# The first MLP layer of a perceiver block computed by Strassen's scheme

## The chip, the cores and the metric

The kernel runs on one core of one Trainium2 chip. The metric is the device time of one execution in microseconds (us). A core has five engines with queues of their own: TensorE (PE) multiplies matrices and writes to PSUM, with its weight loads shown apart as PEld; VectorE (DVE) and ScalarE (ACT) do elementwise work and read PSUM; GpSimd (POOL) does elementwise work in SBUF and issues gathering DMAs; SyncE (SP) issues the plain DMAs. The program writes out one list of instructions for each of them, and in the trace each engine takes its list in order: an instruction that waits holds up all that stand behind it on its engine.

## The reference

All data is float32. Thirty-two batches have 32 query rows of 512 each, and 257 context rows each.

```python
x = x + xattn(layernorm(x), ctx)          # 1: cross attention
x = x + attn(layernorm(x))                # 2: linear attention and an MLP
x = x + ffn(layernorm(x))                 # 3: sum of 8 adapters
# 1: K_hat = cos((ctx @ Wk + bk) @ Wr + br); softmax(Q @ K_hat.T) @ V
# 2: q = x @ Wq; features elu(q) + 1; msg = linear attention @ Wm
x = x + layernorm(msg) * g1 + b1
mlp = relu(msg @ W1) @ W2                 # W1: 512 x 1024, W2: 1024 x 512
x = x + layernorm(mlp) * g2 + b2
# 3: x @ (sum of weights[k] * W[ids[k]]).T + bias, W[i]: 512 x 512
```

`msg @ W1` is the product that the change touches. It has 1024 rows (32 batches of 32), an inner size of 512 and 1024 columns.

## The kernel before, in words

The 1024 query rows are eight groups of 128 rows (four batches each), called g = 0 to 7. The program is written out as 96 **slots**, numbered 8w + u for w in 0 to 11 and u in 0 to 7 (L1130 to L1156). Each slot emits a main piece, and around it pieces from two hand-written plans: `ahead` (L1063) puts a call in front of the slot's main piece and `at` (L1060) behind it. Since every queue is in order, these lists set the order on all engines; each slot's pieces also sit in the queues of DVE, ACT, POOL and SP.

The main pieces are: slots 0 to 63, the keys of the cross attention, two batches per four slots; 64 to 71, the first MLP layer for groups 0 to 3 (`hidden`, L969); 72 to 79, the second layer for these groups (`mlp`, L989); 80 to 87 and 88 to 95 the same for groups 4 to 7. Behind the main pieces, each group's own chain is strewn over some 30 slots: `q_*` (layer norm and query projection), `a_*` (attention, with `a_values` the value projection `xa` and `a_norm` the next layer norm), `b_*` (linear attention: `b_q`, `b_feat`, `b_turn_f`, `b_pairs`, `b_msg`, `b_merge`, `b_turn_m2`), then `mlp_norm` and `f_*`. The last group's chain lies in slots 64 to 80.

Between layers, a 128x512 result must be transposed. For groups 0 to 6 `move` (L261) sends it through four SP DMAs of 64 KB into a `moved` tile, and DVE transposes that in 32x32 blocks (`turn_moved`, L272); the last group goes over PE (`turn`, L245).

**Keys.** Two batches' keys are one product of a 512x512 matrix and a 512x512 matrix, and `pair_unit` (L560) computes it by Strassen's scheme in Winograd's form: seven products of 256x256 blocks instead of eight. `product` (L513) is one of them, four matmuls of 128x128 by 128x256 (in the trace eight instructions: every float32 matmul shows as two). Sums of weight blocks stand in `s_in` (made once, L481), sums of context blocks (`y_sum`, L498) in a tile `sums`, and partial results in a tile `parts`. Three PSUM banks take turns (`z_tile`, L113): bank a collects P1, P6, P7 and P4 one after the other, and is copied out to `parts` in between, so each product waits for a copy made one product earlier.

**First MLP layer.** `hidden(half, f)` computes 128 of the 1024 columns for 512 rows: four matmuls of 128x128 by 128x512 into one bank, then one ReLU on ACT into a tile of the pool `kh` (six buffers, which held the keys). The input `m2T[half]` holds the four groups' `m2` transposed. `m2T[1]` holds the key sums `s_in` until the last keys are done. W1 lies in two tiles `w1_0` and `w1_1` of the pool `stage` (three buffers; the other is the adapters' sum), loaded by SP in slots 34 to 42 and 63 to 66 (L1122 to L1127).

**Adapters.** `adapter_load(m)` (L666) gathers half an adapter, 512 KB, by POOL into buffers of the old context tiles; `adapter_add(m)` (L684) adds it, weighted, to `acc` on DVE; `adapter_move` and `adapter_turn` transpose the sum into `wff`, in the buffer of `wkr` (the product of Wk and Wr); `f_times` (L1041) uses it.

Of the kernel before, what the change touches and what calls it, by code (L numbers as in the profile page):

```python
# [9 lines left out]
F32 = mybir.dt.float32  # L10
I32 = mybir.dt.int32
AF = mybir.ActivationFunctionType
ALU = mybir.AluOpType
# [13 lines left out]
def tile_perceiver_block(  # L27
# [35 lines left out]
    nc = tc.nc  # L63
    P = 128
    B, S, D = x.shape
    SK = y.shape[1]
    DC = D // P
# [7 lines left out]
    NG = B // GB  # L75
# [3 lines left out]
    HALF = NG // 2  # L79
# [109 lines left out]
    weights = {}  # L189
# [133 lines left out]
    for e in range(DC):  # L323
# [11 lines left out]
        if e == 3:  # L335

            ps = tr_tile("phase_parts").rearrange("p a n -> p (a n)")
            for a in range(DC):
# [5 lines left out]
                    stop=True,  # L344
# [136 lines left out]
    def key_sums():  # L481

        (w11, w12), (w21, w22) = w_in
        s1, s2, s3, s4 = s_in
        nc.vector.tensor_tensor(s1, w21, w22, ALU.add)
        nc.vector.tensor_tensor(s2, s1, w11, ALU.subtract)
        nc.vector.tensor_tensor(s4, w12, s2, ALU.subtract)
        nc.vector.tensor_tensor(s3, w11, w21, ALU.subtract)
        sums = stage.tile([P, 3, 2, K0], F32, tag="stage", name="sums")
        parts = stage.tile([P, 4, 2, K0], F32, tag="stage", name="parts")  # L490
        pair_tiles["sums"] = [sums[:, i] for i in range(3)]
        pair_tiles["parts"] = [parts[:, i] for i in range(4)]

    def y_blocks(b):
        ya, yb = turned_y[b], turned_y[b + 1]
        return (ya[:, :2, :], yb[:, :2, :]), (ya[:, 2:, :], yb[:, 2:, :])

    def y_sum(b, i):  # L498

        if b >= B:  # L500
            return
        (y11, y12), (y21, y22) = y_blocks(b)
        t1, t2, t4 = pair_tiles["sums"]
# [462 lines left out]

    hid = {}

    def hidden(half, f):  # L969

        if f % 2 == 0:
            hid[half, f // 2] = khp.tile(
                [P, 2, HALF * P], F32, tag="kh", name=f"hid_{half}_{f // 2}"
            )
        ps = z_tile(f"hid_ps_{half}_{f}")
        for c in range(DC):
            nc.tensor.matmul(  # L977
                ps,
                lhsT=weights[f"w1_{f // 4}"][:, c, (f % 4) * P : (f % 4 + 1) * P],
                rhs=m2T[half][:, c, :],  # L980
                start=(c == 0),
                stop=(c == DC - 1),
            )
        nc.scalar.activation(hid[half, f // 2][:, f % 2, :], ps, AF.Relu)  # L984
        flush_sines()

    mlp_ps = {}

# [71 lines left out]
    def at(w, u, f, *args):  # L1060
        plan.setdefault((w, u), []).append((f, args))

    def ahead(w, u, f, *args):  # L1063

        early.setdefault((w, u), []).append((f, args))

    for g in range(NG):
        for j in range(GB):
            at(g + (5 + j) // 8, (5 + j) % 8, load_plain, g, [j])
        at(g + 1, 1, load_last, g)  # L1070
        if g:
            ahead(g + 0, 0, q_stats, g)
            ahead(g + 0, 5, q_norm, g)
        ahead(g + 1, 0, q_turn, g)
        at(g + 1, 0, q_times, g)
        w = g + 1
        if g == NG - 1:
            steps = (a_scores, a_turn_p, a_sum, a_turn, a_values, a_norm, b_turn)
            steps += (b_q, b_feat, b_turn_f, b_pairs, b_msg, b_turn_msg, b_merge)
            for u, f in enumerate(steps):  # L1080
                at(w + (u + 1) // 8, (u + 1) % 8, f, g)
            at(w + 1, 7, b_stats, g)
            at(w + 2, 0, b_norm, g)
# [3 lines left out]
        if g < NG - 2:  # L1087
            pass
        else:
            steps.update({b_q: 10, b_pairs: 14, b_msg: 15, b_merge: 18})  # L1090
            first.update({b_feat: 12, b_turn_f: 14, b_turn_msg: 17, b_turn_m2: 21, b_stats: 20, b_norm: 21})
# [5 lines left out]
    at(6, 4, adapter_fetch)  # L1097
    at(7, 0, adapter_start)
    at(7, 3, adapter_bias_load)
    at(8, 2, adapter_bias)  # L1100
    for m in range(2 * NK):
        at((60 + m) // 8, (60 + m) % 8, adapter_load, m)
        ahead((64 + m) // 8, (64 + m) % 8, adapter_add, m)
    for c in range(OP):
        at((79 + c) // 8, (79 + c) % 8, adapter_move, c)
        ahead((81 + c) // 8, (81 + c) % 8, adapter_turn, c)
    for g in range(2, NG):
        at(g - 2, 3 if g == 2 else 2, load_x, g)
    for g in range(NG - 3):
        u = 72 + 2 * g + 1 if g < HALF else 88 + 2 * (g - HALF) + 1  # L1110
        steps = {mlp_norm: u + 1, f_stats: u + 2, f_norm: u + 3, f_turn: u + 5, f_times: u + 6}
        if g < HALF:
            u = 80 + 2 * g
            steps.update({f_stats: u, f_norm: u + 1, f_turn: u + 3, f_times: u + 5})
        for f, u in steps.items():
            if (f, g) != (f_times, HALF):
                at(u // 8, u % 8, f, g)
# [4 lines left out]
    for i in range(2):  # L1122
        src = aw1[:, i * D : (i + 1) * D]
        parts += [(f"w1_{i}", src, stage, "stage", [q]) for q in range(4)]
    at_units = (2, 3, 4, 4, 9, 10, 11, 12, 18, 19, 20, 26, 34, 35, 36, 42, 63, 64, 65, 66)
    for part, u in zip(parts, at_units):
        at(u // 8, u % 8, load_weight, *part)  # L1127
    for q in range(4):
        at(8, 3 + q, load_w2, q)
    for w in range(12):  # L1130
        for u in range(8):
            if (w, u) == (8, 0):
                last_fraction()
            for f, args in early.get((w, u), ()):
                f(*args)
            if w < 8:
                b = w * GB + u // 2
                if b == 1:
                    turn_quads(2 + u % 2)
                    load_quads(4 + u % 2)  # L1140
                    if u % 2:
                        y_sum(2, 1)
                        y_sum(2, 2)
                    keys(1, u % 2)
                elif b > 1:
                    pair_unit(w * GB + u // 4 * 2, u % 4)
            elif w == 8:
                hidden(0, u)
            elif w == 9:
                mlp(u // 2, u % 2)  # L1150
            elif w == 10:
                hidden(1, u)
# [73 lines left out]
```

## Time and profile before

| what | value |
|---|---|
| median of 3 runs (lowest, highest) | 532.01 us (531.39, 532.18) |
| profiled execution: its own time | 531.07 us |
| its span, first to last instruction | 529.3 us |
| granted TensorE clock | 1.000 |
| slots 0 to 63 (start of the span to first `hid_ps` matmul) | 346.6 us |
| first MLP layer, groups 0 to 3, with the pieces between | 346.6 to 400.5 us |
| second layer, groups 0 to 3, with the pieces between | 401.0 to 442.2 us |
| first layer, groups 4 to 7, with two `ff` pieces | 442.2 to 476.6 us |
| all 128 `hid_ps` matmul instructions, busy | 57.1 us |
| all 16 ReLUs on ACT | 9.5 us |
| DVE busy in 364 to 378 us / in 442 to 476 us | 5.34 of 14 / 15.72 of 34 us |
| DMA share in 346 to 364 us / in 364 to 378 us | 0.91 / 0.68 |

The page of a profile gives the engines' busy time, the chain of work that ended last (followed back from the last instruction), and the costliest groups of instructions: line, engine, operation, tile written <- tiles read, shapes, count | busy us, mean ns of one | idle time before them and what ended it. The timeline gives start, length, engine, line and operation, merged where like follows like. The name `w` stands for tiles with numbers cut off: `w1_0`, `w1_1` and `w2`.

### The profile page before, as it was taken

The page shows a single profiled execution, that of the slowest core. Times are in us where ns is not written, and L with a number is a line of the kernel's source. Part 1 is how long each engine was busy: PE and PEld are TensorE (multiplying, and loading weights), DVE is VectorE, ACT ScalarE, POOL GpSimd, SP SyncE. Part 2 cuts the span into 40 slices and gives each one's busy share as a digit, 9 for nine tenths or more (in the row PEclk, how much of TensorE's full clock was granted, in tenths as well). Part 3 has the DMA queues.
Part 4 walks back from the last instruction along what each step waited for, and adds up shares of the span by engine and source line. Part 5 has one row for each costly group of instructions (what it writes and reads, how often), then busy time and mean ns, then how long its engine had stood idle before and what let it go on. Part 6 is the DMA issues. An engine that isn't in the chain of part 4 may idle for free.

```text
span 529.3 us, 8651 instructions
## 1 busy us (share of the span) xinstructions
PE 523.7 (99%) x3231; PEld 339.0 (64%) x3231; DVE 361.8 (68%) x621; ACT 205.2 (39%) x405; POOL 145.9 (28%) x164
## 2 busy tenths in 40 slices
PE   8999999999999999999999999999999999999997
PEld 6587877767867766767687676664444444444444
DVE  1498888779877887887887798573535667524473
ACT  0154674574573464456447346443212101110000
POOL 0012111311310420331143043226115776311331
PEclk9999999999999999999999999999999999999999
DMA  7659986557346465453623532578636321211002
GB/s 205 159 142 231 257 199 225 151 149 240 97 127 171 166 167 171 148 169 94 230 83 93 176 129 82 178 193 192 194 120 198 93 62 48 59 40 61 20 20 79
DMA packets 83857, 74.33 MB, mean 140 GB/s; under 512 B 7828, under 2 KB 69792, under 8 KB 83816
## 3 DMA queue, kind: packets, MB, share of 16 engines
q1 hardware_dynamic: 80928, 64.06, 42.7%
q0 software_dynamic: 2864, 9.73, 6.4%
q8 instruction: 25, 0.41, 0.3%
q14 instruction: 16, 0.13, 0.1%
q10 hardware_dynamic: 24, 0.01, 0.0%
HBM read 58.03 MB, written 2.10 MB: 114 GB/s over the span
## 4 chain that ended last, share of the span: by engine, by line
PE 95%; DVE 2%; DMA 1%; SPq 0%; issue 0%; POOL 0%; ACT 0%; DVEq 0%; POOLq 0%
PE a L517 20%; PE hid_ps L977 11%; PE mlp L996 10%; PE b L517 9%; PE q L753 5%; PE ff L283 5%; PE bq L283 5%; PE m L283 5%; PE xa L283 5%; PE c L517 5%; PE sc L771 3%; PE av L802 3%; PE wkr L312 3%; PE msg L910 2%; DMA quads<-in_ctx_dram 1%; PE pa L888 1%
## 5 line engine op out<-in xcount | busy, mean ns | idle before, releaser
L977 PE MATMUL hid_ps<-m2T,w 128*128 128x512 f32 x128 | 57.1, 596 | 0.2 <-issue 0.2
L537 ACT ACTIVATE parts<-kh,rounder 128x512 f32<-128x512 f32 x60 | 43.2, 720 | 36.3 <-DVE kh L534 35.8
L996 PE MATMUL mlp<-w,hid 128*128 128x512 f32 x128 | 56.9, 594 | 0.0
L541 DVE SCALAR_TENSOR_TENSOR kh<-parts,kh 128x512 f32<-128x512 f32 x60 | 42.1, 701 | 9.0 <-ACT parts L537 8.9
L550 ACT ACTIVATE kh<-kh 128x512 f32<-128x512 f32 x60 | 36.3, 627 | 29.8 <-DVE kh L542 29.6
L977 PEld LDWEIGHTS hid_ps<-m2T,w 128*128 128x128 f32 x128 | 23.8, 190 | 29.6 <-issue 29.6
L996 PEld LDWEIGHTS mlp<-w,hid 128*128 128x128 f32 x128 | 23.8, 190 | 27.9 <-issue 27.3
L379 DVE STREAM_TRANSPOSE yT<-quads 128x1024 f32<-128x1024 f32 x31 | 38.2, 1232 | 2.3 <-DMA quads<-in_ctx_dram 2.3
L239 POOL TENSOR_TENSOR rstd_n<-ve_n,mhalf 128x1 f32<-128x1 f32 x16 | 11.1, 692 | 83.4 <-DVE ve_n L237 83.3
L753 PEld LDWEIGHTS q<-hT,wq_sb 128*128 128x128 f32 x256 | 29.8, 192 | 3.5 <-issue 2.6
L517 PE MATMUL a<-sums,wkr 128*128 128x256 f32 x120 | 29.2, 386 | 1.0 <-DVE kh L534 1.0
L984 ACT ACTIVATE hid<-hid_ps 128x512 f32<-128x512 f32 x16 | 9.5, 596 | 53.1 <-PE hid_ps L977 53.1
L753 PE MATMUL q<-hT,wq_sb 128*128 128x128 f32 x256 | 29.9, 275 | 0.0
L517 PE MATMUL a<-yT,m2T 128*128 128x256 f32 x120 | 29.6, 389 | 0.0
L239 POOL TENSOR_TENSOR rstd_x<-ve_x,mhalf 128x1 f32<-128x1 f32 x8 | 7.7, 963 | 78.3 <-DVE ve_x L237 78.3
L529 ACT ACTIVATE parts<-a,turn 128x256 f32<-128x256 f32 x60 | 25.0, 468 | 10.1 <-PE a L517 9.3
L517 PE MATMUL a<-yT,wkr 128*128 128x256 f32 x120 | 28.9, 384 | 0.0
L283 PE MATMUL bq<-awq_sb,bhT 128*128 128x512 f32 x64 | 28.8, 592 | 0.0
L283 PE MATMUL m<-awm_sb,msgT 128*128 128x512 f32 x64 | 28.8, 592 | 0.0
L283 PE MATMUL xa<-wv_sb,aoT 128*128 128x512 f32 x64 | 28.8, 592 | 0.0
L283 PE MATMUL ff<-wff,h2T 128*128 128x512 f32 (+2 forms) x80 | 28.6, 509 | 0.0
L517 PE MATMUL a<-sums,m2T 128*128 128x256 f32 x120 | 28.4, 379 | 0.0
(196 smaller groups left out, 980.4 us busy)
## 6 DMA issues: line engine op xcount, KB each, us to landing
quads<-in_ctx_dram SPq DMA_DIRECT2D x128, 128.0 KB, 3.3
plain<-in_ctx_dram SPq DMA_DIRECT2D x32, 512.0 KB, 4.1
moved_h<-h SPq DMA_DIRECT2D x52, 64.0 KB, 2.2
x<-in_x_dram SPq DMA_DIRECT2D x8, 256.0 KB, 4.0
last<-in_ctx_dram SPq DMA_DIRECT2D x32, 64.0 KB, 2.1
w<-in_L_attn_W_dram SPq DMA_DIRECT2D x8, 256.0 KB, 4.8
w<-in_L_attn_W_dram SPq DMA_DIRECT2D x4, 512.0 KB, 3.4
moved_ao<-ao SPq DMA_DIRECT2D x28, 64.0 KB, 2.2
```

What stands on the lines that cost most here:

```text
L239: nc.gpsimd.tensor_tensor(rstd, ve, mhalf, ALU.pow)
L283: nc.tensor.matmul(ps, lhsT=srcT[:, c, :], rhs=w[:, c, :], start=(c == 0), stop=(c == n - 1))
L312: nc.tensor.matmul(acc[c], lhsT=wkT[:, e, c * P : (c + 1) * P], rhs=wr_sb[:, e, :], start=(e == 0), stop=(e == DC - 1),)
L379: nc.vector.transpose(t.rearrange("p c (n k) -> p n c k", k=32), quads.pop(b))
L517: nc.tensor.matmul(ps[:, o, :], lhsT=w[:, c, o * P : (o + 1) * P], rhs=yb[:, c, :], start=start and o == 0 and c == 0, stop=stop and o == ...
L529: nc.scalar.activation(dst[:, o, :], ps[:, o, :], AF.Identity, bias=turn0[:, r : r + 1], scale=INV_2PI)
L537: nc.scalar.activation(w, u, AF.Identity, bias=rounder)
L541: nc.vector.scalar_tensor_tensor(u, w, ROUNDER, u, ALU.subtract, ALU.subtract)
L550: nc.scalar.activation(u, u, AF.Sin, scale=-TURN)
L753: nc.tensor.matmul(ps[:, e, :], lhsT=wq_sb[:, d, e * P : (e + 1) * P], rhs=hT[:, d, :], start=(d == 0), stop=(d == DC - 1),)
L977: nc.tensor.matmul(ps, lhsT=weights[f"w1_{f // 4}"][:, c, (f % 4) * P : (f % 4 + 1) * P], rhs=m2T[half][:, c, :], start=(c == 0), stop=(c ...
L996: nc.tensor.matmul(ps, lhsT=hT, rhs=weights["w2"][:, f // 2, f % 2, :], start=(f == 0), stop=(f == FC - 1),)
```

## The change

`hidden` is replaced by `hidden_unit(half, k, u)`: for each half of the rows and each half k of W1's columns (a 512x512 by 512x512 product), four slots hold seven products, two in each of u = 0, 1, 2 and one in u = 3. Results go through DVE additions and ReLUs in place. For this, sums of W1's blocks (`w1_sum`, four per k) and of the input's blocks (`m2_sum`, four per half) are made on DVE. `sums` and `parts` of the keys are kept, so the pool `stage` has only one buffer left, for W1's first half. W1's second half goes to two `kh` buffers that held the last keys (`w1_load`); the sums for k = 0 to `wq_sb`, which needs the last `q_times` to be over (moved from slot 64 to 60); the adapters' sum to `wkr`'s buffer, and `wff` to `awq_sb`. Names in order of the slots:

- `w1_sum(0, 1..4)` in slots 61 and 62; `m2_sum(0, 1..4)` in 63 and 64; all four `w1_load` in 66 (before: `w1_1` in 63 to 66); `w1_sum(1, 1..4)` in 67 and 68; `m2_sum(1, 1..4)` in front of 80.
- Group 7: `q_stats` 56 to 52, `q_norm` 61 to 57, `q_turn` and `q_times` 64 to 60, `b_stats` 79 to 82, `b_norm` 80 to 83.
- Group 6: `b_feat` 68 to 67, `b_turn_f` and `b_pairs` 70 to 69, `b_msg` 71 to 70, `b_turn_msg` 73 to 71, `b_merge` 74 to 73, `b_stats` 76 to 75, `b_norm` 77 to 76.
- Adapters: loads 60 to 75 become 59 to 62 and 66 to 77; additions 4 to 15 stay in 68 to 79; moves 79 to 82 become 79, 80, 80, 81. The bias product goes from 66 to 68.
- `f_stats`, `f_norm` and `f_turn` of groups 0 to 3 come one slot later; `f_times` 85, 87, 89, 91 become 85, 88, 91, 94.

```diff
+    def w1_load(q):
+        if q == 0:
+            for i in range(2, 4):
+                hidden_tile(0, i)
+            for i in range(2):
+                w1_late.append(khp.tile([P, 2, D], F32, tag="kh", name=f"w1_1_{i}"))
+        v = aw1[:, D:].rearrange("(q c i) n -> q i c n", q=4, c=DC)
+        for i in range(2):
+            nc.sync.dma_start(
+                out=w1_late[i][q * 32 : (q + 1) * 32, :, :], in_=v[q][:, 2 * i : 2 * i + 2, :]
+            )
...
+        if i == 1:
+            nc.vector.tensor_tensor(s1, w21, w22, ALU.add)
+        elif i == 2:
+            nc.vector.tensor_tensor(s2, s1, w11, ALU.subtract)
+        elif i == 3:
+            nc.vector.tensor_tensor(s3, w11, w21, ALU.subtract)
+        else:
+            nc.vector.tensor_tensor(s4, w12, s2, ALU.subtract)
...
+        def add(dst, ps, p):
+            nc.vector.tensor_tensor(dst, ps, p, ALU.add)
+            relus.append(dst)
+        if u == 0:
+            product(a, w11, y11, stop=False)
+            product(c, w12, y21)
+            nc.scalar.copy(part[0], a)
+        elif u == 1:
+            product(a, s2, t2, start=False, stop=False)
+            product(d, s1, t1, stop=False)
+            add(h[0][0], c, part[0])
+            nc.scalar.copy(part[1], a)
+            nc.scalar.copy(part[2], d)
+        elif u == 2:
+            product(a, s3, y12, start=False, stop=False)
+            product(d, s4, y22, start=False)
+            add(h[1][1], a, part[2])
+            add(h[0][1], d, part[1])
+        else:
+            product(a, w22, t4, start=False)
+            flush_relus()
+            nc.scalar.activation(h[1][0], a, AF.Relu)
+    def flush_relus():
+        while relus:
+            t = relus.pop(0)
+            nc.scalar.activation(t, t, AF.Relu)
...
-            ad["acc"] = stage.tile([P, OP * D], F32, tag="stage", name="acc")
+            ad["acc"] = one.tile([P, OP * D], F32, tag="wkr", name="acc")
...
-            ad["wff"] = one.tile([P, DC, D], F32, tag="wkr", name="wff")
+            ad["wff"] = weights["awq_sb"]
...
+            u = 8 * g + 8 if g < NG - 1 else 8 * g + 4
+            ahead(u // 8, u % 8, q_turn, g)
+            at(u // 8, u % 8, q_times, g)
```

More of the change, by code (lines that the diff above doesn't have):

```diff
@@ L492, in key_sums @@
         pair_tiles["parts"] = [parts[:, i] for i in range(4)]
+        pair_tiles["all_parts"] = parts
     def y_blocks(b):
@@ L502, in y_sum, with block_sum @@
         (y11, y12), (y21, y22) = y_blocks(b)
+        block_sum(y11, y12, y21, y22, i)
+    def block_sum(y11, y12, y21, y22, i):
         t1, t2, t4 = pair_tiles["sums"]
@@ L967, in tile_perceiver_block @@
     hid = {}
[L969 to L973, printed above, removed]
-            )
[L975 to L985, printed above, removed]
+    w1_late = []
@@ new lines, in w1_load, with w1_blocks @@
+    def w1_load(q):
[8 more added lines that the diff above has]
+                out=w1_late[i][q * 32 : (q + 1) * 32, :, :], in_=v[q][:, 2 * i : 2 * i + 2, :]
+            )
+    def w1_blocks(k):
+        if k:
+            halves = w1_late
+        else:
+            halves = [weights["w1_0"][:, 2 * j : 2 * j + 2, :] for j in range(2)]
+        return [[halves[j][:, :, i * 256 : (i + 1) * 256] for j in range(2)] for i in range(2)]
@@ new lines, in tile_perceiver_block, with w1_sum @@
+    w1_sums = {}
+    def w1_sum(k, i):
+        (w11, w12), (w21, w22) = w1_blocks(k)
+        if k not in w1_sums:
+            if k:
+                spare = tmp.tile([P, 1, D], F32, tag="round", name="w1_spare", bufs=1)
+                homes = [wq_sb[:, 3, :], pair_tiles["all_parts"][:, 3], spare[:, 0, :]]
+                homes[1] = homes[1].rearrange("p c n -> p (c n)")
+            else:
+                homes = [wq_sb[:, n, :] for n in range(3)]
+            s1, s2, s4 = [t.rearrange("p (c n) -> p c n", c=2) for t in homes]
+            w1_sums[k] = [s1, s2, w21, s4]
+        s1, s2, s3, s4 = w1_sums[k]
+        if i == 1:
[4 more added lines that the diff above has]
+            nc.vector.tensor_tensor(s3, w11, w21, ALU.subtract)
+        else:
+            nc.vector.tensor_tensor(s4, w12, s2, ALU.subtract)
@@ new lines, in m2_blocks, with m2_sum, hidden_tile, hidden_unit @@
+    def m2_blocks(half):
+        t = m2T[half]
+        return [
+            [t[:, 2 * i : 2 * i + 2, j * 256 : (j + 1) * 256] for j in range(2)] for i in range(2)
+        ]
+    def m2_sum(half, i):
+        (y11, y12), (y21, y22) = m2_blocks(half)
+        block_sum(y11, y12, y21, y22, i)
+    def hidden_tile(half, i):
+        hid[half, i] = khp.tile([P, 2, HALF * P], F32, tag="kh", name=f"hid_{half}_{i}")
+    def hidden_unit(half, k, u):
+        pt = pair_tiles
+        (w11, w12), (w21, w22) = w1_blocks(k)
+        (y11, y12), (y21, y22) = m2_blocks(half)
+        s1, s2, s3, s4 = w1_sums[k]
+        t1, t2, t4 = pt["sums"]
+        part = pt["parts"]
+        if u == 0:
+            for i in range(2):
+                if (half, 2 * k + i) not in hid:
+                    hidden_tile(half, 2 * k + i)
+            for i, key in enumerate("acb"):
+                t = z_tile(f"hid_{key}_{half}_{k}", (B // 2 - 1 + 2 * half + k + i) % 3)
+                pt[key] = t.rearrange("p (o k) -> p o k", o=2)
+        a, c, d = pt["a"], pt["c"], pt["b"]
+        h = [
+            [hid[half, 2 * k + i][:, :, j * 256 : (j + 1) * 256] for j in range(2)]
+            for i in range(2)
+        ]
+        def add(dst, ps, p):
+            nc.vector.tensor_tensor(dst, ps, p, ALU.add)
+            relus.append(dst)
+        if u == 0:
+            product(a, w11, y11, stop=False)
[12 more added lines that the diff above has]
+            add(h[0][1], d, part[1])
+        else:
+            product(a, w22, t4, start=False)
+            flush_relus()
+            nc.scalar.activation(h[1][0], a, AF.Relu)
@@ L987, in tile_perceiver_block @@
+    relus = []
+    def flush_relus():
+        while relus:
+            t = relus.pop(0)
+            nc.scalar.activation(t, t, AF.Relu)
     mlp_ps = {}
@@ L1065, in ahead, with at_slot, ahead_slot @@
         early.setdefault((w, u), []).append((f, args))
+    def at_slot(n, *args):
+        at(n // 8, n % 8, *args)
+    def ahead_slot(n, *args):
+        ahead(n // 8, n % 8, *args)
+    slots = dict(load0=59, load4=66, add0=64, add4=68, wff=81, f=81, ft=85, fd=3, w1_late=66, w1_later=66, w2=67, s0=61, s1=67, t1=63, t3=64, v1=80, v3=80, bias=68)
+    last = (65, 66, 67, 68, 69, 70, 71, 72, 73, 74, 75, 76, 77, 78, 82, 83)
+    six = dict(b_q=10, b_pairs=13, b_msg=14, b_merge=17, b_feat=11, b_turn_f=13, b_turn_msg=15, b_turn_m2=21, b_stats=19, b_norm=20)
     for g in range(NG):
@@ L1071, in tile_perceiver_block @@
         if g:
[L1072 to L1075, printed above, removed]
+            u = 8 * g if g < NG - 1 else 8 * g - 4
+            ahead(u // 8, u % 8, q_stats, g)
+            ahead((u + 5) // 8, (u + 5) % 8, q_norm, g)
+        u = 8 * g + 8 if g < NG - 1 else 8 * g + 4
+        ahead(u // 8, u % 8, q_turn, g)
+        at(u // 8, u % 8, q_times, g)
         w = g + 1
@@ L1079, in tile_perceiver_block @@
             steps += (b_q, b_feat, b_turn_f, b_pairs, b_msg, b_turn_msg, b_merge)
[L1080 to L1083, printed above, removed]
+            steps += (b_stats, b_norm)
+            for u, f in zip(last, steps):
+                at_slot(u, f, g)
             continue
@@ L1086, in tile_perceiver_block @@
         first = {a_turn: 7, a_norm: 9, b_turn: 10, b_feat: 13, b_turn_f: 14, b_turn_msg: 20, b_stats: 23, b_norm: 26, b_turn_m2: 31}
[L1087 to L1091, printed above, removed]
+        if g == NG - 2:
+            for names in (steps, first):
+                names.update({f: six.get(f.__name__, u) for f, u in names.items()})
         for f, u in steps.items():
@@ L1099, in tile_perceiver_block @@
     at(7, 3, adapter_bias_load)
-    at(8, 2, adapter_bias)
+    at_slot(slots["bias"], adapter_bias)
     for m in range(2 * NK):
-        at((60 + m) // 8, (60 + m) % 8, adapter_load, m)
-        ahead((64 + m) // 8, (64 + m) % 8, adapter_add, m)
+        at_slot(slots["load0"] + m if m < 4 else slots["load4"] + m - 4, adapter_load, m)
+        ahead_slot(slots["add0"] + m if m < 4 else slots["add4"] + m - 4, adapter_add, m)
     for c in range(OP):
-        at((79 + c) // 8, (79 + c) % 8, adapter_move, c)
-        ahead((81 + c) // 8, (81 + c) % 8, adapter_turn, c)
+        at_slot(slots["add4"] + 11 + (c + 1) // 2, adapter_move, c)
+        ahead_slot(slots["wff"] + c, adapter_turn, c)
     for g in range(2, NG):
@@ L1112, in tile_perceiver_block @@
         if g < HALF:
-            u = 80 + 2 * g
-            steps.update({f_stats: u, f_norm: u + 1, f_turn: u + 3, f_times: u + 5})
+            u = slots["f"] + 2 * g
+            steps.update({f_stats: u, f_norm: u + 1, f_turn: u + 3})
+            steps.update({f_times: slots["ft"] + slots["fd"] * g})
         for f, u in steps.items():
@@ L1121, in tile_perceiver_block @@
     parts += [("awm_sb", awm, None, None, [q]) for q in range(4)]
[L1122 to L1125, printed above, removed]
+    parts += [("w1_0", aw1[:, :D], stage, "stage", [q]) for q in range(4)]
+    at_units = (2, 3, 4, 4, 9, 10, 11, 12, 18, 19, 20, 26, 34, 35, 36, 42)
     for part, u in zip(parts, at_units):
@@ L1128, in tile_perceiver_block @@
     for q in range(4):
-        at(8, 3 + q, load_w2, q)
+        at_slot(slots["w2"] + q, load_w2, q)
+        at_slot(slots["w1_late"] if q < 2 else slots["w1_later"], w1_load, q)
+    for i in range(1, 5):
+        n = (i - 1) // 2
+        at_slot(slots["s0"] + n, w1_sum, 0, i)
+        at_slot(slots["s1"] + n, w1_sum, 1, i)
+        at_slot(slots["t3" if n else "t1"], m2_sum, 0, i)
+        ahead_slot(slots["v3" if n else "v1"], m2_sum, 1, i)
     for w in range(12):
@@ L1147, in tile_perceiver_block @@
             elif w == 8:
-                hidden(0, u)
+                hidden_unit(0, u // 4, u % 4)
             elif w == 9:
@@ L1151, in tile_perceiver_block @@
             elif w == 10:
-                hidden(1, u)
+                hidden_unit(1, u // 4, u % 4)
             else:
```

## The prediction

> **What bounds the kernel now.** I read the page's busy times first, then the chain that ended last, then the costliest groups.
>
> ```profile
> PE 523.7 (99%) x3231; PEld 339.0 (64%) x3231; DVE 361.8 (68%) x621; ACT 205.2 (39%) x405; POOL 145.9 (28%) x164
> ...
> PE 95%; DVE 2%; DMA 1%; SPq 0%; issue 0%; POOL 0%; ACT 0%; DVEq 0%; POOLq 0%
> ...
> L977 PE MATMUL hid_ps<-m2T,w 128*128 128x512 f32 x128 | 57.1, 596 | 0.2 <-issue 0.2
> ```
>
> PE is busy in 523.7 of 529.3 us and is 95% of the chain. In the first MLP layer it hardly idles (0.2 us), so PE work taken out there shortens the run, unless a wait takes its place. The granted clock is 1.000 throughout. The PE timeline gives the price of the old and the new shape:
>
> ```profile
> 327.92 1.89 PE L517 MATMUL a<-yT,wkr 128*128 128x256 f32 x8
> 329.65 1.89 PE L517 MATMUL c<-yT,wkr 128*128 128x256 f32 x8
> 331.38 1.89 PE L517 MATMUL a<-sums,m2T 128*128 128x256 f32 x8
> 333.10 1.89 PE L517 MATMUL b<-sums,m2T 128*128 128x256 f32 x8
> ...
> 442.22 20.76 PE L977 MATMUL hid_ps<-m2T,w 128*128 128x512 f32 x48
> 462.82 3.60 PE L283 MATMUL ff<-wff,h2T 128*128 128x512 f32 x8
> ```
>
> Starts count, since lengths overlap. Six old units last 462.82 - 442.22 = 20.60 us, 3.433 each; a product lasts (333.10 - 327.92) / 3 = 1.727 us.
>
> **1. The products.** Removed: 16 units of 3.433 = 54.93 us. Added: 2 halves x 2 k x 7 products = 28 of 1.727 = 48.36 us. On PE: **-6.57 us**. Weight loads rise from 128 to 224, 190 ns each by the group of L517, below the 216 ns between two instructions of a product, so they stay hidden.
>
> **2. Elementwise work.** DVE gets 16 sums at 0.68 (row `sums<-yT,sums` of L507: 677 ns) and 12 additions from PSUM at 0.69 (L534), 19 us. ACT gets 12 copies at 0.59 (7 us); ReLUs stay 16. The keys' loop already shows this cadence: a copy or an addition stands under the next product (1.73 us), and PE idles 1.0 us in all its 105 products. DVE has room: busy 5.34 of 14 us in 364 to 378, 15.72 of 34 us in 442 to 476. Cost on PE 0 while the queues run ahead; the places where they may not follow.
>
> **3. Start of slots 64 and 65.** `q_times(7)` (3.57 us) moves to slot 60, so slots 61 to 64 begin 3.57 us later and slot 65 at 357.1 as before. P6 there needs bank a copied out. That copy stands on ACT behind the Sin of the last keys, that behind DVE's f21. Walking DVE's queue with its rows (`b_stats` at 348.2, 1.0; two transposes, f22, the zsum reductions: 352.1; two new sums 1.4; f12 and f21 2.1), f21 ends near 355.5, Sin and copy (0.6 each) near 356.8. P6 follows at 357.15: margin 0.35. I take 0; bound 0 to 0.7, one sum.
>
> **4. `bq` of group 6.** Its input now comes late: `xa` of group 6 ends at 357.1 instead of 353.56 while `bq` stays at 367.1. Between: update 0.75, statistics 1.0, two new sums 1.6 (L511: 930 ns, and 683), `bh` 0.55: 361.0. Then four SP issues of 0.62 (2.49), the last issued at 362.9 and landed 2.2 later (median of `moved_bh`): 365.1; DVE, with one normalisation and the reductions of `sc` in front, transposes (1.1) until 366.9 at most, against 367.1. With the landing of 7.0 that the group had at 358 us, when the DMA share was 0.91, it would end at 371.0, late by 3.9; W1's second half no longer loads in that time. I take 0.2, range 0 to 3.9, nearer the median.
>
> **5. W1's second half: the new wait.** The old loads came in slots 63 to 66 and had until slot 68. The new ones must wait for the last keys to be read (`sc` ends at 363.6) and stand on SP behind what these lines show:
>
> ```profile
> 356.96 2.49 SPq L266 DMA_DIRECT2D moved_bh<-bh  x4
> 362.54 3.33 SPq L266 DMA_DIRECT2D moved_msg<-msgs  x4
> 365.91 2.08 SPq L168 DMA_DIRECT2D last<-in_ctx_dram  x4
> 368.03 0.90 SPq L201 DMA_DIRECT2D w<-in_L_attn_W_dram  x2
> ```
>
> So they start at about 368.1: eight issues of 0.45, the last at 371.3, 1.05 MB. PE reaches slot 68, which reads them, after `bq` and `tr_p` (370.85), P4 (1.73) and `av` (1.86) at **374.5**. Lower bound of the landing: 3.3 (median of 128 KB `quads`), 374.6, wait 0. Upper: 11.4, the longest of the trace (512 KB `plain` in 347 to 350 us, 2.5 MB together): 382.7, wait 8.2. Between them decides what else loads. POOL gathers half adapters at the same time:
>
> ```profile
> 366.80 2.12 POOL L957 TENSOR_TENSOR x<-x,n 128x512 f32<-128x512 f32 x1
> 369.08 0.98 POOL L676 DMA_INDIRECT adapter<-in_L_ffn_W_dram,ido  x1 [0.15 <-issue]
> 370.36 0.94 POOL L676 DMA_INDIRECT adapter<-in_L_ffn_W_dram,ido_odd  x1 [0.30 <-issue]
> ```
>
> After the change three (loads 4, 5, 6) can start at 369.1, 370.4, 371.7, 0.5 MB each; load 7 stands behind a normalisation of slot 69. At the 219 GB/s of 346 to 364 us (share 0.91), W1 plus half of the gathers (1.05 + 0.75 MB) takes 8.2 us: 376.3; at the 264 GB/s read in 370 to 375 us, 374.9. I take a wait of **1.5 us** (376.0). The sums for k = 1 follow on DVE by 377.4, P6 of slot 69 needs them after 381: covered. Behind the waiting sum on DVE stand `msgT` of group 5 (needed in slot 70) and an adapter addition: no reader on PE before 381.
>
> **6. `pa` of group 6**, one slot earlier, needs a transpose on DVE behind the bias copy and two sums: 0.69 x 3 + 1.1 = 3.2 us after `bff`, while PE has P6 and P5, 3.45. Margin 0.25; I take 0.2, range 0 to 1.3 (one adapter addition, 1.28, in between).
>
> **7. Second half, slots 80 to 87.** No foreign PE work lies between the products except one `ff`. From the end of `mlp` 3: statistics 1.1, t1 and t2 1.4: 2.5 us, P6 follows at 3.45. The addition that frees bank a for P4 (slots 83, 87) has 1.73 us from P7's end and takes 0.7; the transposes of `wff` (1.05 each) before it end by 8.6 where P7 ends at 8.65. Cost 0, up to 2 if POOL or a landing holds one of them.
>
> A rule of the Trainium skill speaks against these sums. The trace shows an adapter addition of L692 taking 2.62 us at 415.53, median 1.28, beside POOL's additions at 415.79 and 417.14. The page "SBUF — State Buffer", section "Who interferes with whom", says that a DVE instruction with two SBUF inputs and a GpSimd instruction that reads SBUF exclude each other for a whole instruction. By it, one POOL addition of 1.27 in front of t2 would turn the margin of 0.95 into a wait of 0.3; the forecast would be 527.6.
>
> **8. Adapters.** `acc` waits for P4 of slot 63, which DVE's f21 awaits anyway. Loads 7 to 15 have two slots instead of four; the last is issued near 431, lands 5.7 later (median), its addition ends near 438.5; moves (2.5 of issue, 2.2 landing) and transposes are done before `ff` 0 near 458. Cost 0; 0 to 2 if a landing takes 8.0. **The tail** from 476 on keeps its PE work, 0; a spaced-out `ff` 3 puts its output DMA (2.0) before `n2` of group 7, with 1.3 us to spare.
>
> **Sum**: -6.57 + 1.5 + 0.2 + 0.2 = -4.7 us on the profiled execution's 531.07 (span 529.3, 1.8 around it): 526.4. The median of the runs shown, 532.01, is 0.94 above that execution: **527.3 us**.
>
> **Rivals.**
> - *W1 lands in time* and every margin holds: -6.57, 532.01 - 6.6 = **525.4**. For it: 128 KB DMAs land in 3.3 and the 264 GB/s row leaves 0.4 us. Against: three gathers start in the same 3 us.
> - *The queues become the bound.* DVE and ACT do not keep up where margins are 0.2 to 0.4: points 3, 4, 6 and 7 cost half their upper ends, 0.35 + 1.95 + 0.65 + 1.0 = 3.95, on top of 1.5: 532.0 - 6.6 + 5.45 = **530.9**. For it: DVE was busy 18.7 of 20 us in 300 to 320. Against: PE was busy throughout those 20 us.
> - *Slower: W1's second half lands as late as `plain` did.* 11.4 us from the last issue is a wait of 8.2 in slot 68: 532.0 - 6.6 + 8.2 + 0.4 = **534.0**. It passes no change when the wait exceeds 6.2 us, a landing after 380.7. For it: 2.6 MB are wanted within 4 us, as then. Against: the earlier 2.5 MB were all plain loads in one queue, and here W1 is ahead of most of the gathers.
> - *It doesn't do what it says*: the compiled products could need the same PE time, if 256 columns cost more than half of 512. The keys' rows above (1.727 against 3.433 / 2 = 1.717) exclude it; no chance is given.
>
> **How the numbers follow.** Forecast 0.50, in time 0.28, queues 0.12, late W1 0.10. About 0.2% (1.06 us) is what a measurement of this kernel can tell from no change. The late case is slower in most of its spread (0.08) and same in 0.02; the queues case lies at the edge of no change: faster 0.06, same 0.05, slower 0.01. So faster 0.50 + 0.28 + 0.06 = 0.84, same 0.07, slower 0.09. The range: the in-time case less 0.4 of run-to-run spread, 525.0, to the queues case, 530.9; outside lie the late case and some of both ends, under 2 in 10.
>
> **What would show it.** Right: some 224 matmul instructions at the products' line in the hidden slots, spaced 216 ns; slot 72 near 399 and slot 80 near 439; one idle of PE of 0.5 to 3 us before the first product of k = 1 in half 0, released by the DMA of W1's second half; no idle over 0.3 us in slots 80 to 87. Wrong: PE waiting there for DVE or ACT instead, `bq` of group 6 waiting for its transpose, or W1 landing after 378.

## The result, and the profile after

The changed kernel took a median of 532.9 us (22 runs, 531.3 to 534.5), the kernel before on the same chip 531.85 us (22 runs, 530.9 to 532.7). The ratio is 1.0020, with a 95% interval of 1.0011 to 1.0029: slower by a little, where 527.3 us was forecast. The profiled execution after has a span of 531.7 us against 529.3 us, 2.4 us more. The kernel before ran again beside the experiments; each ratio below is against its runs on the same chip.

The page of the changed kernel: busy times, granted clock in 40 slices, and the engines' shares of the chain that ended last.

```profile
PE 520.0 (98%) x3327; PEld 359.2 (68%) x3327; DVE 380.2 (71%) x649; ACT 211.6 (40%) x417; POOL 145.9 (27%) x164
...
PEclk9999999999999999999999999999799999999999
...
PE 91%; DMA 4%; DVE 3%; SPq 1%; POOL 1%; issue 0%; ACT 0%; DVEq 0%; POOLq 0%
```

PE has 3.7 us less to do than before (523.7), not 6.6, in a longer span. One slice, at 372 to 385 us, has a clock of 0.7, and DMA has risen from 1% to 4% of the chain. The PE timeline of the same kernel shows where (start, length, engine, line, operation, tiles, shapes, count, and in brackets the idle time before it and what ended it):

```profile
370.82 1.89 PE L521 MATMUL hid_a<-sums,w 128*128 128x256 f32 x8
372.71 1.92 PE L806 MATMUL av<-plain,pT 128*32 128x512 f32 x16
381.15 3.75 PE L521 MATMUL hid_a<-m2T,w 128*128 128x256 f32 x8 [6.52 <-DMA w<-in_L_attn_W_dram]
384.70 2.35 PE L521 MATMUL hid_c<-m2T,w 128*128 128x256 f32 x8
386.88 0.60 PE L249 MATMUL tr_ao<-ident,ao 128*128 128x128 f32 x4
...
406.61 3.60 PE L1094 MATMUL mlp<-w,hid 128*128 128x512 f32 x8
...
447.81 1.89 PE L521 MATMUL hid_a<-m2T,w 128*128 128x256 f32 x8
...
466.80 3.60 PE L283 MATMUL ff<-awq_sb,h2T 128*128 128x512 f32 x8
470.24 1.89 PE L521 MATMUL hid_a<-m2T,w 128*128 128x256 f32 x8
...
475.42 3.60 PE L1094 MATMUL mlp<-w,hid 128*128 128x512 f32 x8
```

PE stood still for 6.52 us in slot 68, in front of the first product of k = 1 in half 0, until W1's second half landed. Then two products that last 1.73 us elsewhere took 384.70 - 381.15 = 3.55 and 386.88 - 384.70 = 2.18 us. The windows of two microseconds around it (time, PE busy with its count, granted clock, DMA share, GB/s) show why:

```profile
374.00:376.00 2.00, 0.63 (x8) 1.00 1.10 205
376.00:378.00 2.00, 0.00 (x0) 1.00 1.00 260
378.00:380.00 2.00, 0.00 (x0) 0.70 1.04 295
380.00:382.00 2.00, 0.85 (x2) 0.50 1.12 248
382.00:384.00 2.00, 2.00 (x6) 0.50 1.07 270
384.00:386.00 2.00, 2.00 (x7) 0.60 1.05 409
386.00:388.00 2.00, 2.00 (x11) 1.00 0.31 111
```

While PE stood, the clock fell to a half and came back at 385.6 us or so. The two products took 1.82 + 0.45 = 2.27 us more for it, all on the path. The DMA engines were full from 374 us on (share 1.00 and more). What filled them, by the DMA issues of this stretch (KB of each, median us from issue to landing, where the view has one):

```profile
w<-in_L_attn_W_dram SPq DMA_DIRECT2D x8, 128.0 KB, 7.7
w<-in_L_attn_W_dram SPq DMA_DIRECT2D x3, 512.0 KB, 6.9
last<-in_ctx_dram SPq DMA_DIRECT2D x4, 64.0 KB, 1.9
moved_f<-f SPq DMA_DIRECT2D x4, 64.0 KB
adapter<-in_L_ffn_W_dram,ido POOLq DMA_INDIRECT x2, 9.2
adapter<-in_L_ffn_W_dram,ido_odd POOLq DMA_INDIRECT x1, 9.5
```

The eight of 128 KB are W1's second half, the three of 512 KB are quarters of W2 (issued from 378.08 on). The start times are in SP's and POOL's timelines:

```profile
363.87 2.48 SPq L266 DMA_DIRECT2D moved_msg<-msgs  x4
366.70 1.73 SPq L168 DMA_DIRECT2D last<-in_ctx_dram  x4
368.55 3.64 SPq L985 DMA_DIRECT2D w<-in_L_attn_W_dram  x8
```

```profile
369.19 1.01 POOL L680 DMA_INDIRECT adapter<-in_L_ffn_W_dram,ido  x1 [0.16 <-issue]
370.50 0.94 POOL L680 DMA_INDIRECT adapter<-in_L_ffn_W_dram,ido_odd  x1 [0.30 <-issue]
371.75 0.94 POOL L680 DMA_INDIRECT adapter<-in_L_ffn_W_dram,ido  x1 [0.31 <-issue]
```

W1's first part was issued 0.6 us ahead of the first gather and its last beside the third; all of W1 had landed at 380.9 us, about when the gathers' last bytes moved. How the two streams shared the engines is in the rows of the DMA queues for 375 to 380 us (packets, MB, share of the engines' time; q0 carries POOL's gathers, q1 the loads of SP):

```profile
q0 software_dynamic: 237, 0.87, 69.0%
q1 hardware_dynamic: 233, 0.39, 34.4%
```

The queues moved as many packets as each other, but those of the gathers were over twice as large, so W1's queue got a third of the engines' time and moved 0.39 MB in 5 us, 78 GB/s, against the 219 GB/s that step 5 had taken for all queues together. The sum of the profiled execution is -6.57 (products) + 6.52 (wait) + 2.27 (clock) = +2.2 us, against +2.4 in the spans.

The Trainium skill bears on both. Its page "DMA: Bandwidth & Descriptors", section "Queues, rings and completion order", says that each DMA engine takes packets in turn from the queues that have work. The rows of the queues fit it: 237 packets of one queue and 233 of the other, in the same 5 us. The page "TensorE: Matmul & The Clock Gate", section "What's actually happening", gives a halved clock behind an idle window of about 3.4 us, and full clock after as long a stretch of work. The 0.50 behind the 6.52 us agrees, and full clock came back 4.5 us after PE began again; for shorter waits see the last section.

### The profile page after: what moved, and what is told of

Read it like the earlier page. It is cut to its first block, busy times and chain, and to the rows that moved or that the text cites. A ratio compares the mean times of both kernels' runs of the same rounds, so it can differ in the third digit from the quotient of the medians.

```text
span 531.7 us, 8887 instructions
## 1 busy us (share of the span) xinstructions
PE 520.0 (98%) x3327; PEld 359.2 (68%) x3327; DVE 380.2 (71%) x649; ACT 211.6 (40%) x417; POOL 145.9 (27%) x164
## 4 chain that ended last, share of the span: by engine, by line
PE 91%; DMA 4%; DVE 3%; SPq 1%; POOL 1%; issue 0%; ACT 0%; DVEq 0%; POOLq 0%
PE a L521 19%; PE mlp L1094 10%; PE b L521 9%; PE q L757 5%; PE xa L283 5%; PE ff L283 5%; PE m L283 5%; PE hid_a L521 5%; PE c L521 5%; PE bq L283 5%; PE wkr L312 3%; PE sc L775 2%; PE av L806 2%; PE hid_b L521 2%; DMA w<-in_L_attn_W_dram 2%; PE hid_c L521 1%
## 5 line engine op out<-in xcount | busy, mean ns | idle before, releaser
L239 POOL TENSOR_TENSOR rstd_n<-ve_n,mhalf 128x1 f32<-128x1 f32 x16 | 10.0, 627 | 88.7 <-DVE ve_n L237 88.7
L283 PE MATMUL ff<-awq_sb,h2T 128*128 128x512 f32 (+2 forms) x80 | 28.5, 507 | 0.0
L521 PE MATMUL b<-yT,m2T 128*128 128x256 f32 x120 | 28.3, 379 | 0.0
L521 PE MATMUL c<-yT,wkr 128*128 128x256 f32 x120 | 28.3, 379 | 0.0
L521 PE MATMUL b<-sums,m2T 128*128 128x256 f32 x120 | 28.3, 379 | 0.0
```

The lines of the kernel that those rows point to most:

```text
L239: nc.gpsimd.tensor_tensor(rstd, ve, mhalf, ALU.pow)
L283: nc.tensor.matmul(ps, lhsT=srcT[:, c, :], rhs=w[:, c, :], start=(c == 0), stop=(c == n - 1))
L521: nc.tensor.matmul(ps[:, o, :], lhsT=w[:, c, o * P : (o + 1) * P], rhs=yb[:, c, :], start=start and o == 0 and c == 0, stop=stop and o == ...
```

## The experiments

Three theories stood at the start. **A**: W1's second half is issued late, shares the DMA engines with three gathers, and PE's standing still costs clock on top. **B**: these 128 KB loads are slow by themselves. **C**: the gain is lost to the additions and sums on DVE.

**W1 sooner (e1).** The loads go into slot 65, right behind `sc`, the last reader of their buffers. With that, `moved_msg` and the last row of ctx (`load_last(7)`) stand behind them on SP.

```diff
-        at_slot(slots["w1_late"] if q < 2 else slots["w1_later"], w1_load, q)
...
+    (msg5, last7, sc7) = plan[(8, 1)]
+    plan[(8, 1)] = [sc7] + [(w1_load, (q,)) for q in range(4)] + [msg5, last7]
```

> Edit: in slot 65 the last scores and the loads of W1's second half come in front of the messages of group 5, so on SP these eight loads stand before the moves of the messages and the last keys. Theory A (the loads start late on SP and then share the DMA engines with three gathers, and TensorE stands still for them): they start near 363.5 instead of 368.5 us, the gathers start at 369 as before, so most of W1 has landed by then; the idle of 6.5 us in slot 68 and the half clock behind it (2.2 us) go: about 6.5 us under before, 525.4. Theory B (these 128 KB loads onto 32 partitions need over 7 us whatever else runs): landing 7 us after the issue of each, the last near 374.5, wait 0 to 1, 525.5 to 526.5, with landings near 7. Theory C (the gain was lost to the added additions and sums on VectorE, and the wait only took the place of others): other idle of TensorE appears, and the time stays within 2 us of the changed kernel.

Measured: 530.17 us (526.5 to 532.8), ratio 0.9968, interval 0.9948 to 0.9989. DMA issues and PE timeline of its profiled execution (own time 526.6 us):

```profile
w<-in_L_attn_W_dram SPq DMA_DIRECT2D x8, 128.0 KB, 3.2
last<-in_ctx_dram SPq DMA_DIRECT2D x4, 64.0 KB, 4.4
```

```profile
374.35 1.99 PE L521 MATMUL hid_a<-m2T,w 128*128 128x256 f32 x8
376.18 1.89 PE L521 MATMUL hid_c<-m2T,w 128*128 128x256 f32 x8
379.05 0.66 PE L249 MATMUL tr_ao<-ident,ao 128*128 128x128 f32 x4 [0.97 <-DVE ao L817]
```

The same eight loads land in 3.2 us when no gather runs beside them, and the wait is gone: B falls. But the 525.4 of theory A was missed. Only the profiled execution has a clock of 1.000; the other eleven have 0.990 to 0.997, and ten of them take 1.4 to 6.2 us more. Something else seems to make PE wait in them. The profiled one hints at it: `tr_ao` waits 0.97 us, through `ao` on DVE, for the last row, which now lands in 4.4 us instead of 1.9.

**Gathers later (e2).** W1 stays where the change put it; the gathers that ran beside it move away, and their additions with them.

```diff
+    loads = (59, 60, 61, 62, 69, 69, 70, 71, 72, 73, 73, 74, 75, 75, 76, 77)
+    adds = (64, 65, 66, 67, 72, 72, 73, 73, 74, 75, 75, 76, 77, 78, 78, 79)
...
-        at_slot(slots["load0"] + m if m < 4 else slots["load4"] + m - 4, adapter_load, m)
-        ahead_slot(slots["add0"] + m if m < 4 else slots["add4"] + m - 4, adapter_add, m)
+        at_slot(loads[m], adapter_load, m)
+        ahead_slot(adds[m], adapter_add, m)
```

> Edit: gathers 4 to 15 of the adapters go to slots 69 to 77 and their additions to slots 72 to 79; W1's loads stay where the change has them. Theory A: without the three gathers the eight loads, issued from 368.5 to 372.2, land some 3.5 to 4 us after their issue, the last near 376; TensorE waits 1 to 2 us, the clock stays at 1.00; 5 us under before, about 526.8. Theory B: they land after 7 to 8 us as in the changed kernel, the wait is 5 us or more and the clock falls: 530 to 532. Theory C: within 2 us of the changed kernel.

Measured: 529.98 us (527.0 to 533.2), ratio 0.9978, interval 0.9958 to 0.9997. The PE timeline of its profiled execution:

```profile
375.00 1.97 PE L521 MATMUL hid_a<-m2T,w 128*128 128x256 f32 x8 [0.64 <-DMA w<-in_L_attn_W_dram]
...
444.69 1.97 PE L521 MATMUL hid_a<-sums,wq_sb 128*128 128x256 f32 x8 [1.59 <-DVE sums L511]
```

With W1 issued as late as in the changed kernel (368.4 us) but no gather beside it, the wait is 0.64 us. So the gathers, not the late issue alone, make the 6.5 us. The edit has a price at the other end: the last addition is now late, and the sums of slot 80 with it. The 526.8 of theory A was met only by the fastest executions: eight of the twelve have clocks of 0.994 to 0.997, and which wait they had was not seen; e4 below shows the wait of slot 80 at a length at which the clock falls.

**PE kept busy (e3).** 24 matmuls of 128x128, whose results nobody reads, stand in front of the first product of k = 1 in half 0. They add work and take none away.

```diff
+        if (half, k, u) == (0, 1, 0):
+            idle_matmuls(24, "idle_w1")
```

> Edit: 24 matmuls of 128x128 by 128x128 on the identity, whose result nobody reads, are put on TensorE in front of the first product of k = 1 in half 0, where it stands still for W1. Theory A with the clock as a loss of its own: they take about 5 us of the 6.5 us wait, W1 lands as late as before, but the granted clock stays at 1.00 and the two products behind the wait take 1.73 us each again instead of 3.55 and 2.17: 2.2 us under the changed kernel, about 530.7. If the clock reading cost nothing, the time stays at 532.9.

Measured: 533.15 us (530.85 to 535.56), ratio 1.0031, interval 1.0013 to 1.0048. The PE timeline of its profiled execution (535.46 us):

```profile
374.29 5.62 PE L299 MATMUL idle_w<-ident 128*128 128x128 f32 x48
380.52 1.97 PE L521 MATMUL hid_a<-m2T,w 128*128 128x256 f32 x8 [0.60 <-DMA moved_f<-f]
382.41 1.97 PE L521 MATMUL hid_c<-m2T,w 128*128 128x256 f32 x8
...
415.35 2.67 PE L1096 MATMUL mlp<-w,hid 128*128 128x512 f32 x4 [2.66 <-DMA w<-in_L_attn_W_dram]
```

The two products behind the filler take 1.89 and 1.80 us instead of 3.55 and 2.18, at a clock of 1.00, beside DMA engines as full as before: the clock fell because PE stood. (The 0.60 us is put down to `moved_f`, which stands behind W1 on SP and which the product does not read.) The time won was not kept. In this profile the fourth quarter of W2, which stands on SP behind the moves of slot 70, was issued at 407.31 and landed 8 us later beside three gathers, so PE stood for 2.66 us there and the clock fell again. Two other executions look like this one (535.2 and 535.6 us, clock 0.997). The remaining seven have clocks of 0.999 and 1.000 and still a median of 532.7: where their gain went is not shown. On the total the run is a miss; on the clock it decides.

**Both edits (e4).** The two edits of e1 and e2 together.

> Both edits of the first two runs: W1's loads ahead on SP, gathers 4 to 15 later. Theory A: W1 lands near 370 us, no wait; as fast as the first run, 525.4, and less if some wait for W1 was left there. Theory B: landings still near 7 us, no wait either. Theory C: within 2 us of the changed kernel. A gather or addition that comes too late would show as a wait of the adapters' transposes in slots 81 to 85.

Measured: 528.13 us (527.4 to 529.4), ratio 0.9939, interval 0.9922 to 0.9956. No load makes PE wait between 360 and 390 us. One wait is left, the one that e2's later gathers brought:

```profile
440.12 1.89 PE L521 MATMUL hid_c<-m2T,w 128*128 128x256 f32 x8
444.69 3.56 PE L521 MATMUL hid_a<-sums,wq_sb 128*128 128x256 f32 x8 [2.68 <-DVE sums L511]
448.09 1.89 PE L521 MATMUL hid_b<-sums,wq_sb 128*128 128x256 f32 x8
```

A wait of 2.68 us costs 4.4: the product behind it takes 3.40 instead of 1.73.

**W2's fourth quarter and the last gathers (e5, e6).** What still delayed most executions of e1? e5 takes e1 and issues W2's fourth quarter a slot sooner; e6 adds the last four gathers, a slot sooner each.

```diff
-        at_slot(slots["w2"] + q, load_w2, q)
+        at_slot(slots["w2"] + min(q, 2), load_w2, q)
...
-        at_slot(slots["load0"] + m if m < 4 else slots["load4"] + m - 4, adapter_load, m)
+        at_slot(slots["load0"] + m if m < 4 else slots["load4"] + m - 4 - (m > 11), adapter_load, m)
```

> The kernel of e1 (W1's second half issued in slot 65) with one more edit: the fourth quarter of W2 is issued in slot 69, not in slot 70. Open after e1 to e4: which later wait makes e1's executions spread from 526.5 to 532.8 us. Theory F (the fourth quarter of W2 is late): in e3's profile it landed 8.0 us after its issue, beside three gathers, and the second MLP layer stood 2.66 us in slot 72 with the clock at 0.57 behind it, some 4.5 us together. Issued before 385 us it has 20 us and more, so the executions draw together, the median falls to 526 to 528 and the mean granted clock of nearly all is 0.999 or 1.000. Theory G (the last gather's addition holds DVE ahead of the sums of slots 79 and 80): nothing changes against e1, median 529.5 to 531, clocks 0.990 to 0.997 as before.

> The kernel of e5 with one more edit: the last four gathers (12 to 15) are issued one slot sooner each, the last one in slot 76 ahead of the normalisations, with the additions where they were. The last gather is then issued near 424 instead of 434 us and has landed before 434, so that its addition in slot 79 waits for nothing and slot 80's first products find their sums. Theory F alone: as e5, within 0.3 us. Theory G alone: e5 stays at 529.5 to 531, e6 falls to 526 to 528 with clocks of 0.999 to 1.000. Both: each takes a part, e6 ends at 525.5 to 527, and its executions spread by no more than 2 us, as those of the kernel before do.

Measured: e5 531.24 us (530.0 to 533.3), ratio 1.0003 (0.9989 to 1.0018); e6 530.65 us (526.9 to 533.0), ratio 0.9990 (0.9971 to 1.0010). As causes of the spread, both theories, F and G, failed. The profile of e5 shows what both had missed (PE timeline):

```profile
375.35 1.89 PE L521 MATMUL hid_c<-m2T,w 128*128 128x256 f32 x8
380.62 1.11 PE L249 MATMUL tr_ao<-ident,ao 128*128 128x128 f32 x4 [3.38 <-DVE ao L817]
381.67 2.07 PE L712 MATMUL bff_ps<-bsel,w_cb 8*128 8x512 f32 x2
383.67 3.61 PE L521 MATMUL hid_a<-sums,parts 128*128 128x256 f32 x8
```

It is the hint of e1 at full size. The waits of DVE in 365 to 385 us name the transfer:

```profile
DVE ao L817 <- DMA last<-in_ctx_dram: 6.2, 1, 6.2
```

The last row of ctx, 64 KB in each of four loads, landed 6.8 us after its issue: e1's edit issues it behind W1, here from 369.90, when the first gather was already out (366.79). W1 had been saved at the cost of the row.

**The last row first (e7, e8, e9).** The row's buffer is free from slot 61 on, so it can be issued in slot 62. e8 is the changed kernel with this edit alone; e7 is e6 with it; e9 is e1 with it (W2 and the gathers as in the change), so e9 against e1 shows what the row alone does.

```diff
-        at(g + 1, 1, load_last, g)
+        at(*((g + 1, 1) if g < NG - 1 else (7, 6)), load_last, g)
```

> The kernel of e6 with one more edit: the last row of ctx of group 7 (a 64 KB load read by ao in slot 67), which e1, e5 and e6 issue behind W1's second half, is issued in slot 62, ahead of everything that loads from 363 us on. Theory A, extended after e5 and e6: between 363 and 380 us about 4 MB share one set of DMA engines and whatever is issued last of what PE needs by 376 us is late; in e1, e5 and e6 that was this row (landing 4.4, 6.8 and 5.8 us; tr_ao stood 0.97, 3.4 and 1.5 us in the profiled executions, and the clock fell behind it). With the row out of the way nothing that PE needs by 385 us is behind the gathers: no wait of PE over 0.6 us between 350 and 480 us, clock 0.999 or 1.000 in most executions, median 525.5 to 527.0, spread no more than 2.5 us. Rival H (the executions spread for another cause, the gathers or the order on DVE): the median stays at 529.5 to 531 with clocks of 0.993 to 0.997.

> The changed kernel with only this edit: the last row of ctx of group 7 is issued in slot 62 instead of slot 65, so that four issues (1.7 us) fewer stand ahead of W1's second half on SP; W1 stays in slot 66 and begins to issue at about 366.7 instead of 368.55 us. Theory A: the three gathers still start from 369.2 us, in the middle of W1's issues, so W1 lands between 375 and 379: a wait of 0.5 to 4.5 us in slot 68, clock below 1 behind it in most executions, median 528.5 to 531.5. Rival (the delay on SP alone matters, not what else loads): the wait shortens by just the 1.8 us, from 6.5 to 4.7, and the median lies at 530.5 to 531.5.

> The kernel of e7 without its two other edits: W2's fourth quarter is back in slot 70 and the last four gathers in their own slots; only W1's second half (slot 65) and the last row (slot 62) are issued sooner than in the changed kernel. It tells what these two edits are worth alone. If the loads of 363 to 380 us are the whole cause: 524 to 525 us, as e7. If W2's fourth quarter or the last gather is late in some executions too (as in e3's and e4's profiled ones): 525 to 527.5 us, with clocks below 0.999 in several executions and a spread of 2 to 5 us.

| kernel | median us (lowest to highest) | ratio (95% interval) | profiled span, clock |
|---|---|---|---|
| e7 (4 executions), W1, last row, W2's quarter and last gathers sooner | 524.26 (523.97 to 525.26) | 0.9855 (0.9840 to 0.9869) | 523.5, 1.000 |
| e9 (4), W1 and the last row sooner | 525.01 (523.62 to 525.68) | 0.9878 (0.9856 to 0.9900) | 523.2, 1.000 |
| e8 (6), the last row sooner, W1 as changed | 526.02 (524.39 to 530.25) | 0.9901 (0.9870 to 0.9931) | 524.3, 1.000 |

PE's waits of e7, the whole run (line waited for, total, times, longest):

```profile
PE idle L299 <- POOL ident masks.py:199: 1.3, 1, 1.3
PE a L521 <- DVE kh L538: 0.8, 1, 0.8
PE msg L914 <- issue: 0.2, 1, 0.2
```

The first two stood in the kernel before too (1.4 and 1.0). Nothing of the change makes PE wait any more in this profile; the four executions lie within 1.3 us, and e7 beats both kernels. The row alone, e9 against e1, takes the ratio from 0.9968 to 0.9878; the clocks, 0.990 to 1.000 in e1, are 0.999 and 1.000 in e9. C falls with it: every added sum and addition is still there. e7 is better than its expectation (525.5 to 527.0); e9 lies on the border of its two (524 to 525, or 525 to 527.5). e9 against e7 tells little, as their intervals overlap: whether W2's quarter and the last gathers are worth anything is open. e8 is better than its expectation (528.5 to 531.5):

```profile
372.30 1.92 PE L806 MATMUL av<-plain,pT 128*32 128x512 f32 x16
375.93 1.96 PE L521 MATMUL hid_a<-m2T,w 128*128 128x256 f32 x8 [1.71 <-DMA w<-in_L_attn_W_dram]
377.73 1.89 PE L521 MATMUL hid_c<-m2T,w 128*128 128x256 f32 x8
```

W1's issues ended 1.8 us sooner (366.61 to 370.41), and it landed 5.2 us sooner, at 375.7: five of its eight issues now lay ahead of the first gather (368.78), against two of eight in the changed kernel. From 368 to 371 us, before the gathers' first bytes moved, SP's queue carried 0.72 MB in e8 and 0.41 MB in the changed kernel; at the 78 GB/s that it got beside the gathers in the changed kernel, the difference is worth some 4 us (an estimate from these rows). The expectation's rival, that SP's delay alone counts, wanted a wait of 4.7 us and falls. The clock stayed at 1.00 behind the 1.71 us. (One of e8's six executions took 530.25 us at a clock of 0.997, so its wait may not always be so short.) This one profile is the forecast's own case: a wait of 1.5 had been priced, and the span is 5.0 us below before's, against the forecast's 4.7.

## Why the prediction was wrong

- **Step 5 failed: W1's second half, "the new wait".** It said "W1 plus half of the gathers (1.05 + 0.75 MB)", landing at 376.0, a wait of 1.5 us. The rate was right and the amount was wrong. All three gathers shared the engines with W1 to the end, and took two thirds of them: 1.05 + 1.5 MB at the same 219 GB/s from 368.1 are 11.6 us, 379.7, a wait of 5.2; measured were 380.9 and 6.5. Step 5 also left out the four `moved_f` (0.26 MB), which were in flight too and are worth up to 1.2 us at that rate. e2 shows it the other way round: without the gathers the same issue gives a wait of 0.64 us.
- **The clock was not priced.** No step said what a wait does to PE behind it. It was 2.27 us here, and by the sum above it carries the result over the line: -6.57 + 6.52 alone would have been no change. e3 shows that it comes from PE standing still.
- **The slower rival is what happened.** Its mechanism (W1 as late as `plain` had been) and its point of decision ("a landing after 380.7") were right: 9.61 us from the issue of the part that landed last (371.30) against its 11.4, landing at 380.9. The reasons given against it were the error. "Here W1 is ahead of most of the gathers": only two of its eight parts were issued ahead of the first gather, and that head start of 0.6 us was too little; e8 and e1 show that a longer one does help. And the earlier loads were not "all plain loads in one queue": in the kernel before, POOL had issued a gather at 346.59, which landed 6.2 us later, beside them.
- **Step 1, the products, was right.** 447.81 to 466.80 are eleven products and 470.24 to 475.42 three: 24.17 us, 1.726 each, against 1.727 forecast. e9, with the waits gone, is 6.5 us below before by its ratio (5.3 to 7.6) against 6.57; e7 is 7.7 below (7.0 to 8.5), some 1 us more than the products explain, and that is not settled: the spans of the profiled executions are only 5.8 (e7) and 6.1 us (e9) below.
- **Steps 2 and 7 (no cost of the sums and additions) were right**: no idle in slots 80 to 87, and DVE's 18 us more show nowhere on PE. A late sum appeared only in e2 and e4, where a gather was moved. **Steps 3, 4 and 8 held too**: slot 65 began at 357.11 and `bq` of group 6 at 367.16 with no wait. Nothing of the rival of the queues was seen in the changed kernel. **Step 6** can't be read there, as the wait of slot 68 gave `pa` time; in e1 it waited 0.81 us for its transpose, within the bound of 1.3, in e7 not at all.
- Slot 72 was to begin near 399 and slot 80 near 439. They began at 406.61 and 447.81 in the changed kernel, late by the wait and the clock; in e7 slot 80 begins at 439.55.

## What to carry to other kernels

When a load gets a later start, price its landing with all that is in flight on every queue until it ends, and ask what share of the engines the other queue takes (here two thirds); what is moved before the other queue starts counts for much more. When it is put forward, ask which load now stands behind it (here the last row of ctx). Price an idle of PE at more than its own length: in these runs a wait of 2.7 us cost 4.4 (e4) and one of 6.5 us cost 8.8 (the changed kernel). If the executions of one kernel suddenly spread by several microseconds with a clock below 1, look for a transfer that is sometimes late; the profile of a fast execution shows at most a hint of it, as the 0.97 us of e1 did.

## What the runs showed of the hardware that was not expected

The clock falls behind waits shorter than 6.5 us. Behind 2.68 us (e4) and 3.38 us (e5) the windows show 0.50 to 0.53, behind 1.71 us (e8) and 1.59 us (e2) 1.00. In e6, `tr_ao` waited 1.52 us, and the product 1.6 us behind it took 3.32 us instead of 1.73. Nor does the clock fall at a fixed moment. Read in windows of 0.25 us, the half clock begins 2.5 us (e4), 2.9 us (e5) and 4.2 us (changed kernel) after PE came to a stand, and in e3's wait for W2 and in e6 only 1.2 and 1.9 us after PE had begun again. It then lasts 3.4 us (e3, e4, e6) or twice that, 6.8 us (changed kernel, e5), whatever the wait. So a length of wait from which the clock falls can't be named from these runs; the idle window of 3.4 us (the Trainium skill, the same page and section as above) is longer than the 2.68 us that were enough here. In e6 the wait lies among short pieces of PE work, and whether these count as idle time was not tried.
